# Layer 1 of a two-layer attention kernel: the last chunk's sums move to TensorE, the value biases move into the residual, and VectorE joins two groups of rows in eight products with addition

## The chip, the cores and the metric

The kernel runs on one core of a Trainium2 chip. A core has a matrix engine (TensorE, PE in the profile, with its weight loads as PEld), a vector engine (VectorE, DVE), a scalar engine (ScalarE, ACT), a general engine (GpSimd, POOL) and SyncE (SP), whose queue issues most transfers here. The metric is device time in microseconds for one execution; smaller is better.

## What is computed

The input x has 2 images of 256 channels on 64 x 64 = 4096 positions, in float32. Two attention layers follow each other.

```python
# layer 0, per image: 4 heads of 16
xn  = layernorm(x)                      # over the 256 channels
att = softmax(q k^T / 4) @ v            # 4096 x 4096 scores per head
att = att * dyn[position]               # a gate from two small products on x
x1  = sigmoid(0.5 * (out_w att) + x)

# layer 1, per image: 4 heads of 64
q, k, v = w_qkv x1 + b_qkv              # v carries a bias of its own
att = softmax(q k^T / 8) @ v            # 4096 x 4096 scores per head
att = att.reshape(256, 4096)            # [head, position, d] read as [channel, position]
out = w_out att + b_out + x1
```

The reshape in layer 1 matters for the change: `(b, heads, position, d)` is read as `(b, channel, position)`. A row of the new 256 x 4096 array holds 64 positions of one head, each with its 64 values, so along the free axis a row repeats the 64 values of d 64 times. The softmax weights of a row add up to 1, so the value bias of head h adds the same 64 numbers to every position of that head.

## The kernel before: how the work is tiled and ordered

Layer 0 is streamed in steps of 128 keys and is not touched beyond its last stage, `finish` (L558): tanh on ScalarE, a scaling on GpSimd (L564), and a store of the finished 128 x 2 x 512 tile of x1 (L565). `layer1_constants` (L178) loads the weights and biases of layer 1 while layer 0 starts.

Layer 1 works in **units** (L769): one image b, one pair of heads g, one block j of 512 query positions. There are 2 x 2 x 8 = 32 units, in one long pipeline. A unit has 32 **chunks** of 128 keys, in two groups of 16; a **step** of the main loop (L1219) takes two chunks, so a unit starts every 16 steps. I call the step inside a unit its phase, 0 to 15. For one chunk and both heads:

- `score` (L850): TensorE makes a 128 x 2 x 512 tile of scores in PSUM (L861). Two such tiles rotate (pool `psp`), so the scores of a chunk wait until the copy of the chunk two before has been made.
- `keep` (L867): VectorE takes the running maximum over chunks (L878), then ScalarE copies the scores into one of 24 buffers in SBUF, the ring (L879).
- Twenty chunks (ten steps) later, when the group's maximum is known, `shift` (L942) subtracts it on VectorE (L944), and `weigh` (L951) takes the exponential on ScalarE (L956). It also adds the tile to the group's accumulator on GpSimd (L966 for the first sum, L968 after it): 15 additions per group of 16 chunks.
- `gather` (L970): TensorE multiplies the tile with the values (L978), into one PSUM bank per group.

Inside a step the program order is written out by hand (L1219 to L1247), and every engine works through its own instructions in that order: both scores; what hangs at "start" and "early"; the first chunk's keep, shift and exponential; what hangs at "early end"; the second chunk's keep; the two gathers; what hangs at "late" and "late end"; the second shift. Other work is hung on phases (L1109 to L1156): transposes of the maxima (L886) at phases 8 and 0, with VectorE's reductions (L898) behind them, their split into parts on GpSimd (L909 to L916), the turn on TensorE (L925) and the spread (L939); queries of the next unit at phases 14 and 15 (L672); keys and values of the next pair of heads at phases 4 to 7, only in the first 24 units.

The end of a unit runs ten steps into the next one. The groups' two halves are joined there:

- `total` (L998), phase 12: four products with ones (L1008) add the accumulators over the partitions, into the one bank `misc` (pool `psm`, one buffer; everything small uses it: keys, values, queries, transposes, output products).
- `factors` (L1029), phase 13: the reciprocal of the sums on VectorE, and a factor for each group.
- `turn_sums` and `rows` (L1042, L1045): the gathered values are transposed (L1023) into `misc`, and VectorE multiplies each by its factor (L1049): group 1 at the end of phase 13, group 0 at "early end" of phase 14. For group 1, GpSimd adds the value bias (L1056). For group 0, GpSimd adds the two halves (L1060; VectorE in the last unit). The rows then go to DRAM (L1076).

In the units that follow the first image, 16 output products hang as well (`project_out` and `output`, L1081 and L1089): TensorE at phases 3, 7, 11 and 15, and VectorE adds the output bias and x1 (L1091) at the end of the same step. The second image's outputs come at the very end, in `project_half` (L1192). For the last 20 chunks of the last unit `on_tensor` (L948) sends most sums to TensorE (L988) in place of GpSimd.

Of the kernel before, what the change touches and what calls it, by code (L numbers as in the profile page):

```python
# [27 lines left out]
def conv_attention_kernel(  # L28
# [57 lines left out]
    )  # L86
    x1 = [
        [dram.tile([C, NB], F32, tag=f"x1_{b}_{j}", name=f"x1_{b}_{j}") for j in range(NJ)]
        for b in range(B)
    ]  # L90
    att = [dram.tile([C, N], F32, tag=f"att_{b}", name=f"att_{b}") for b in range(B)]
# [86 lines left out]
    def layer1_constants():  # L178

        w1 = const.tile([P, CC, 3, C], F32, tag="w1", name="w1")  # L180
        for c in range(CC):
            for k in range(3):
                later_load(
                    w1[:, c, k, :].rearrange("p (h d) -> p h d", d=D1),
                    w_qkvT[c * P : (c + 1) * P, :].rearrange(
                        "p (h t d) -> p t h d", t=3, d=D1
                    )[:, k],
                )
        wo1 = later_load(
            const.tile([P, CC, C], F32, tag="wo1", name="wo1"), w_outT.rearrange(by_chunk, p=P)  # L190
        )

        b1 = const.tile([P, PR, 3], F32, tag="b1", name="b1")
        for k in range(2):
            later_load(
                b1[k * D1 : (k + 1) * D1],
                b_qkv_col.rearrange("d (g k t) -> d g k t", k=2, t=3)[:, :, k, :],
            )
        b1v = later_load(
            const.tile([P, H, D1], F32, tag="b1v", name="b1v"),  # L200
            b_qkv_row.rearrange("(h t d) -> t h d", t=3, d=D1)[2].partition_broadcast(P),
        )
        bo1 = later_load(const.tile([P, CC], F32, tag="bo1", name="bo1"), b_out)
        ident16 = const.tile([P, P], BF16, tag="ident16", name="ident16")
        nc.gpsimd.tensor_copy(ident16, ident)
        ones16 = const.tile([P, P], BF16, tag="ones16", name="ones16")
        nc.gpsimd.memset(ones16, 1.0)
        ones = const.tile([P, D1], F32, tag="ones", name="ones")
        nc.gpsimd.memset(ones, 1.0)


        negmax1 = []
        for i in range(2):
            t = const.tile([P, PB, P], BF16, tag=f"negmax1_{i}", name=f"negmax1_{i}")
            nc.gpsimd.memset(t, 0.0)
            negmax1.append(t)
        return w1, wo1, b1, b1v, bo1, ident16, ones16, ones, negmax1
# [27 lines left out]
    with own0:  # L245
# [306 lines left out]
        def add_x(u, c):  # L552
# [2 lines left out]
                xt[:, c, :], work.pop(("o", c)), gam, xt[:, c, :], ALU.mult, ALU.add  # L555
            ))

        def finish(u):  # L558
            b, j = u
            avs.pop(u)  # L560
            xt = res.pop(u)

            seq(nc.scalar.activation(xt, xt, AF.Tanh, scale=0.5))  # L563
            seq(nc.gpsimd.tensor_scalar(xt, xt, 0.5, 0.5, ALU.mult, ALU.add))  # L564
            nc.sync.dma_start(out=x1[b][j].rearrange("(c p) n -> p c n", p=P), in_=xt)  # L565


        for n, u in enumerate(units0):
# [87 lines left out]


        w1, wo1, b1, b1v, bo1, ident16, ones16, ones, negmax1 = layer1_constants()
        l1o = own1.enter_context(tc.tile_pool(name="l1o", bufs=1, side="right"))
        l1x = own1.enter_context(tc.tile_pool(name="l1x", bufs=2, side="right"))  # L660
        small_bank = [bank]
# [110 lines left out]
    LAG = GS // 2 + 2  # L772
    US = NM // 2
    END = len(units) * US


    LATE = len(units) * NM - 2 * LAG
    with (
# [172 lines left out]
        def weigh(t):  # L951
            u = b, g, j = units[t // NM]
            m = t % NM
            n = m // GS
            p = raws[t]
            seq(nc.scalar.activation(p, p, AF.Exp, scale=D1**-0.5))  # L956

            if on_tensor(t):
                return
            if (u, n) not in first:  # L960
                first[u, n] = p
            elif (u, n) not in accs:
                accs[u, n] = l1.tile(
                    [P, 2, NB], F32, tag="acc", bufs=3, name=f"acc_{b}_{g}_{j}_{n}"
                )
                seq(nc.gpsimd.tensor_tensor(accs[u, n], first[u, n], p, ALU.add))  # L966
            else:
                seq(nc.gpsimd.tensor_tensor(accs[u, n], accs[u, n], p, ALU.add))  # L968

        def gather(t):  # L970
            u = b, g, j = units[t // NM]
            m = t % NM
            n = m // GS
            if m % GS == 0:
                avs1[u, n] = psv.tile([P, NB], F32, tag="av", name=f"av1_{b}_{g}_{j}_{n}")
            v = vs[b, g, m // PB]
            for k in range(2):
                seq(nc.tensor.matmul(  # L978
                    avs1[u, n][k * D1 : (k + 1) * D1, :], v[:, m % PB, k, :], raws[t][:, k, :],
                    start=(m % GS == 0), stop=(m % GS == GS - 1),  # L980
                ))
            raws.pop(t - 1, None)
            if on_tensor(t):
                if u not in srows:
                    srows[u] = psp.tile([P, 2, NB], F32, tag="pair", name="late_sums")[:, 0, :]
                for k in range(2):
                    r = D1 * n + 32 * k
                    seq(nc.tensor.matmul(  # L988
                        srows[u][r : r + 32, :], ones[:, :32], raws[t][:, k, :],
                        start=r not in begun, stop=False, skip_group_check=True,  # L990
                    ))
                    begun.add(r)
            if m % GS == GS - 1:
                a = l1.tile([P, NB], F32, tag="avs", name=f"avs1_{b}_{g}_{j}_{n}")
                seq(nc.scalar.copy(a, avs1.pop((u, n))))
                avs1[u, n] = a

        def total(u):  # L998


            b, g, j = u
            late = u in srows
            if not late:
                srows[u] = misc(f"sum1_{b}_{g}_{j}")
            for n in range(NG):
                for k in range(2):
                    r = D1 * n + 32 * k
                    seq(nc.tensor.matmul(  # L1008
                        srows[u][r : r + 32, :], ones[:, :32], accs[u, n][:, k, :],
                        start=not late, stop=True, skip_group_check=late,  # L1010
                    ))

        def keep_total(u):
# [31 lines left out]
        def rows(u, n):  # L1045
            b, g, j = u
            ps = avs1.pop((u, n))
            r = l1.tile([P, PB, 2, D1], F32, tag="rows", name=f"rows_{b}_{g}_{j}_{n}")
            seq(nc.vector.tensor_tensor(  # L1049
                r, ps, joined[u][:, n].unsqueeze(3).to_broadcast([P, PB, 2, D1]), ALU.mult  # L1050
            ))
            last = u == units[-1]
            if n == 1:
                halves[u] = r
                bias = b1v[:, 2 * g : 2 * g + 2, :].unsqueeze(1).to_broadcast([P, PB, 2, D1])
                seq(nc.gpsimd.tensor_tensor(r, r, bias, ALU.add))  # L1056
                return
            joined.pop(u)
            engine = nc.vector if last else nc.gpsimd
            seq(engine.tensor_tensor(r, r, halves.pop(u), ALU.add))  # L1060


            if last:
# [24 lines left out]

        def output(b, j, o):  # L1089
            xt = loaded["xo", b, j]  # L1090
            seq(nc.vector.scalar_tensor_tensor(  # L1091
                xt[:, o, :], outs.pop((b, j, o)), bo1[:, o : o + 1], xt[:, o, :], ALU.add, ALU.add
            ))
            if o == CC - 1:
                nc.sync.dma_start(
                    out=out[b, :, bass.ts(j, NB)].rearrange("(c p) n -> p c n", p=P), in_=xt
                )

        def fetch_output(b, j):
            fetch(("xo", b, j), x1[b][j], "xo", 2, l1)  # L1100
            fetch(("ao", b, j), att[b][:, bass.ts(j, NB)], "ao", 1, l1)


# [5 lines left out]
        for n, u in enumerate(units):  # L1109
# [37 lines left out]
            if b < B - 1 and (g, j) == (PR - 1, NJ - 1):  # L1147
                for i in range(NJ):
                    t1 = t0 + US + (i + 4) * GS // 2
                    at(t1, "start", lambda b=b, i=i: fetch_output(b, i))  # L1150
                    for o in range(CC):
                        at(
                            t1 + 3 + 4 * o, ("early", "late")[o],
                            lambda b=b, i=i, o=o: project_out(b, i, o, misc(f"o1_{b}_{i}_{o}")),
                        )
                        at(t1 + 3 + 4 * o, "late end", lambda b=b, i=i, o=o: output(b, i, o))  # L1156

# [2 lines left out]
        def fetch_last(i):  # L1162
# [1 line left out]
            b = B - 1  # L1164
            tag, bufs, pool = (("xb", 3, l1x), ("xo", 2, l1), ("ao", 1, l1))[(i >= 3) + (i >= 5)]
            t = pool.tile([P, CC, NB], F32, tag=tag, bufs=bufs, name=f"x_last_{i}")
            nc.sync.dma_start(out=t, in_=x1[b][i].rearrange("(c p) n -> p c n", p=P))
            last_x.append(t)

        def fetch_first_half():  # L1170
# [5 lines left out]
        def last_output():  # L1176
# [9 lines left out]
            last_att.append(a)  # L1186
            for i in range(NJ - 2, NJ):
                t = tail.tile([P, CC, NB], F32, tag=f"xo{i}", name=f"x_last_{i}")
                nc.sync.dma_start(out=t, in_=x1[b][i].rearrange("(c p) n -> p c n", p=P))
                last_x.append(t)  # L1190

        def project_half(j, c, a):  # L1192
            ps = psp.tile([P, 2, NB], F32, tag="pair", name=f"o1_{c}_{j}")
            for o in range(CC):
                seq(nc.tensor.matmul(
                    ps[:, o, :], wo1[:, c, bass.ts(o, P)], a, start=True, stop=True
                ))
            for o in range(CC):
                x = last_x[j][:, o, :]
                if c == 0:  # L1200
                    seq(nc.vector.scalar_tensor_tensor(
                        x, ps[:, o, :], bo1[:, o : o + 1], x, ALU.add, ALU.add
                    ))
                else:
                    seq(nc.vector.tensor_tensor(x, ps[:, o, :], x, ALU.add))

        own_tail = ExitStack()
        for i in range(NJ - 2):
# [96 lines left out]
```

## Time and profile before

| what | value |
|---|---|
| median of 3 runs (lowest to highest) | 4742.49 us (4742.18 to 4742.60) |
| profiled execution: its own time / span of its trace | 4741.58 us / 4739.8 us |
| layer 1's first scores | 2058.0 us from the span's start |
| granted TensorE clock, mean | 0.996 |
| PE busy, whole span | 4526.9 us (96%) |
| VectorE busy, whole span | 3917.0 us (83%) |
| ScalarE busy, whole span | 3394.1 us (72%) |
| GpSimd busy, whole span | 2540.6 us (54%), of which L968 2098.1 us |

Times are microseconds from the start of the span unless marked ns. A group of instructions is one source line on one engine, with its operation and tile sizes; "busy" is the union of its instructions' times and "mean" the time of one. Matmuls appear as two instructions each in float32 (x4 for two products). In a timeline, a row is one instruction or a run of like ones without a pause ("x8"), with the idle time before it and what ended it in brackets. In the chain of waits each row names the work on which the next row waited, and "issue" is time in which nothing that the profile shows was waited for. A releaser is inferred: where an instruction waits for several engines, the profile names the one whose signal came last before the start, whether or not that signal was needed.

### The profile page before, as it was taken

The numbers are of one execution on the slowest core, as the hardware profiler recorded it, in microseconds if no ns is written. First come the engines' busy times: TensorE is split into PE (matmuls) and PEld (weight loads), VectorE is DVE, ScalarE is ACT, GpSimd is POOL, SyncE is SP. The second block draws the span as 40 slices with busy tenths as digits, with TensorE's granted clock in tenths as the row PEclk, the third lists the DMA queues.
The fourth block names the chain that finished last, engine by engine and source line by source line (L and its number), as shares of the span: only waits on it lengthen the run. The fifth ranks groups of instructions, "written<-read, shape, count | busy, mean of one in ns | idle before, by whom it ended". The sixth has DMA issues, their size and how long they took to land.

```text
span 4739.8 us, 70643 instructions
## 1 busy us (share of the span) xinstructions
PE 4526.9 (96%) x27506; PEld 1496.2 (32%) x27506; DVE 3917.0 (83%) x4584; ACT 3394.1 (72%) x4508; POOL 2540.6 (54%) x1491
## 2 busy tenths in 40 slices
PE   8999999999999999989999999999999999999998
PEld 3433333333333333333232232323233332222222
DVE  6777777777777777359999999999999899999996
ACT  3366666666666666668888888888887778888884
POOL 6300000000000000039999999999998889999994
PEclk9999999999999999999999999999999999999999
DMA  3100000000000000110000100001111111000002
GB/s 103 34 4 19 19 21 15 15 15 15 15 15 15 15 13 13 57 63 25 23 25 17 54 30 23 25 23 36 52 36 45 63 52 47 18 14 7 14 16 74
DMA packets 113381, 140.10 MB, mean 30 GB/s; under 512 B 51864, under 2 KB 52696, under 8 KB 112932
## 3 DMA queue, kind: packets, MB, share of 16 engines
q1 hardware_dynamic: 111260, 135.11, 9.2%
q8 instruction: 216, 3.54, 0.3%
q14 instruction: 121, 0.99, 0.1%
q10 hardware_dynamic: 1784, 0.46, 0.0%
HBM read 93.58 MB, written 41.70 MB: 29 GB/s over the span
## 4 chain that ended last, share of the span: by engine, by line
PE 58%; DVE 15%; POOL 15%; issue 6%; ACT 5%; DMA 1%; SPq 0%; ACTq 0%; DVEq 0%; POOLq 0%
PE s L448 24%; POOL acc L968 13%; PE av L463 12%; DVE rmax L878 10%; PE s L861 6%; PE av L978 5%; DVE raw L944 4%; ACT raw L879 4%; PE a L410 2%; PE p L270 1%; PE k1p L672 1%; POOL acc L966 1%; PE rt L886 1%; PE q1p L672 1%; PE o L549 1%
## 5 line engine op out<-in xcount | busy, mean ns | idle before, releaser
L968 POOL TENSOR_TENSOR acc<-acc,raw 128x1024 f32<-128x1024 f32 x884 | 2098.1, 2373 | 89.4 <-ACT raw L956 30.2
L414 DVE TENSOR_REDUCE mx<-a 128x1 f32<-128x512 f32 x2048 | 1315.3, 686 | 450.5 <-PE a L410 449.4
L451 ACT ACTIVATE p<-s 128x512 f32<-128x512 f32 x2048 | 1109.8, 597 | 701.3 <-PE a L410 367.3
L944 DVE TENSOR_TENSOR raw<-raw,shift 128x1024 f32<-128x1024 f32 x1024 | 1238.0, 1213 | 19.2 <-PE shift L939 12.7
L861 PE MATMUL s<-q,k 64*128 64x512 f32 x4096 | 1117.2, 636 | 142.9 <-ACT raw L879 134.6
L878 DVE TENSOR_TENSOR rmax<-s,rmax 128x1024 f32<-128x1024 f32 x960 | 1170.1, 1219 | 72.7 <-PE s L861 70.8
L879 ACT COPY raw<-s 128x1024 f32<-128x1024 f32 x1024 | 1037.7, 1013 | 259.4 <-DVE rmax L878 173.5
L448 PE MATMUL s<-q,kT 32*128 32x512 f32 x4096 | 1219.1, 640 | 0.0
L956 ACT ACTIVATE raw<-raw 128x1024 f32<-128x1024 f32 x1024 | 1086.9, 1062 | 178.4 <-DVE raw L944 147.3
L410 PE MATMUL a<-kT,q 32*128 32x512 f32 x4096 | 1129.7, 643 | 1.2 <-DVE mx L414 1.0
L978 PE MATMUL av<-raw,v 128*64 128x512 f32 x4096 | 999.3, 606 | 2.0
L463 PE MATMUL av<-p,v 128*32 128x256 f32 (+1 forms) x7904 | 650.2, 399 | 0.6 <-ACT avs L477 0.6
L861 PEld LDWEIGHTS s<-q,k 64*128 64x128 f32 x4096 | 317.1, 185 | 827.9 <-ACT raw L879 628.0
L513 POOL TENSOR_TENSOR f<-f,dyn 128x16 f32<-128x16 f32 x15 | 3.3, 223 | 1028.2 <-DVE f L512 1028.2
L448 PEld LDWEIGHTS s<-q,kT 32*128 32x128 f32 x4096 | 397.9, 183 | 426.3 <-issue 392.1
L978 PEld LDWEIGHTS av<-raw,v 128*64 128x64 f32 x4096 | 243.3, 136 | 587.6 <-issue 428.8
L463 PEld LDWEIGHTS av<-p,v 128*32 128x32 f32 x7904 | 157.6, 108 | 751.5 <-issue 737.3
L564 POOL TENSOR_SCALAR res<-res 128x1024 f32<-128x1024 f32 x16 | 16.8, 1049 | 660.5 <-ACT res L563 660.5
L410 PEld LDWEIGHTS a<-kT,q 32*128 32x128 f32 x4096 | 305.0, 184 | 31.4 <-DVE mx L414 18.2
L966 POOL TENSOR_TENSOR acc<-raw,raw 128x1024 f32<-128x1024 f32 x64 | 152.4, 2381 | 112.7 <-ACT raw L956 103.8
L898 DVE TENSOR_REDUCE negs<-rt 128x4 f32<-128x512 f32 x128 | 88.3, 690 | 50.1 <-PE rt L886 47.6
L318 DVE RECIPROCAL std<-std 128x128 f32<-128x128 f32 x64 | 56.1, 920 | 37.7 <-ACT std L313 37.7
(332 smaller groups left out, 1840.4 us busy)
## 6 DMA issues: line engine op xcount, KB each, us to landing
x<-in_x_dram SPq DMA_DIRECT2D x16, 512.0 KB
res<-in_x_dram SPq DMA_DIRECT2D x16, 512.0 KB
x<-res SPq DMA_DIRECT2D x16, 512.0 KB
att<-rows SPq DMA_DIRECT2D x62, 128.0 KB
kd<-k1s SPq DMA_DIRECT2D x24, 256.0 KB
vd<-v1s SPq DMA_DIRECT2D x24, 256.0 KB
k<-kd SPq DMA_DIRECT2D x24, 256.0 KB
v<-vd SPq DMA_DIRECT2D x24, 256.0 KB
```

The source lines that it names most:

```text
L410: seq(nc.tensor.matmul(ps, qs0[u][r, bass.ts(i, P)], kTs[b][r, bass.ts(m, NB)], start=True, stop=True,))
L414: seq(nc.vector.tensor_reduce(mxs[u][:, i * H + h, m : m + 1], ps, AX.X, ALU.max))
L448: seq(nc.tensor.matmul(ps, kTs[b][r, bass.ts(m, P)], qs0[u][r, :], start=True, stop=True))
L451: seq(nc.scalar.activation(pt[:, k, :], ps, AF.Exp, scale=D0**-0.5))
L463: seq(nc.tensor.matmul(avs[u][32 * h : 32 * h + 32, cols], vs0[b][:, m, 32 * h : 32 * h + 32], pts[t, h // 2][:, h % 2, cols], start=(m == ...
L861: seq(nc.tensor.matmul(ps[:, k, :], ks[b, g, m // PB][r, bass.ts(m % PB, P)], qs1[u][r, :], start=True, stop=True,))
L878: seq(nc.vector.tensor_tensor(rmax[u, n], ps, before, ALU.max))
L879: seq(nc.scalar.copy(raw, ps))
L944: seq(nc.vector.tensor_tensor(raws[t], raws[t], shifts[u, t % NM // GS], ALU.add))
L956: seq(nc.scalar.activation(p, p, AF.Exp, scale=D1**-0.5))
L968: seq(nc.gpsimd.tensor_tensor(accs[u, n], accs[u, n], p, ALU.add))
L978: seq(nc.tensor.matmul(avs1[u, n][k * D1 : (k + 1) * D1, :], v[:, m % PB, k, :], raws[t][:, k, :], start=(m % GS == 0), stop=(m % GS == GS ...
```

## The change

Four things change together.

1. The sums of each unit's last chunk (m = 31) leave GpSimd. Two products with ones on TensorE, behind that chunk's gather in phase 10, add it into `misc` directly. The bank is therefore taken at phase 10 and not at phase 12, and `total` adds the accumulators to it.
2. The value bias leaves `rows`. It is multiplied with w_out once, in layer 0 (`make_bias` on TensorE, `keep_bias` on ScalarE, which adds the output bias too), and `finish` stores a second copy of x1 with that bias added (`xb1`; one GpSimd addition of 128 x 1024 and one store of 512 KB per block). The outputs read `xb1`, so that they need only an addition.
3. In `rows`, the two halves are no longer added by GpSimd. Group 0 no longer gets a product and an addition; VectorE makes eight scalar_tensor_tensor instructions of 128 x 64 instead, each a product with a per-partition factor and an addition to group 1's row.
4. The output products of odd blocks move from phases 11 and 15 to 10 and 15, and the first of each two is added at "early end", so that `misc` is free again when the sums take it. In `project_half` two VectorE instructions of 512 become one of 1024.

```diff
+        def make_bias():
+            ps = bank("bias")
+            for o in range(CC):
+                for c in range(CC):
+                    seq(nc.tensor.matmul(
+                        ps[:, bass.ts(o, D1)], wo1[:, c, bass.ts(o, P)], b1v[:, c, :],
+                        start=(c == 0), stop=(c == CC - 1),
+                    ))
...
         def finish(u):
             nc.sync.dma_start(out=x1[b][j].rearrange("(c p) n -> p c n", p=P), in_=xt)
+            xb = l0w.tile([P, CC, NB], F32, tag="xb", bufs=1, name=f"xb1_{b}_{j}")
+            seq(nc.gpsimd.tensor_tensor(
+                xb.rearrange("p c (s d) -> p c s d", d=D1),
+                xt.rearrange("p c (s d) -> p c s d", d=D1),
+                bias.unsqueeze(2).to_broadcast([P, CC, NB // D1, D1]),
+                ALU.add,
+            ))
+            nc.sync.dma_start(out=xb1[b][j].rearrange("(c p) n -> p c n", p=P), in_=xb)
...
         def weigh(t):
-            if on_tensor(t):
+            if on_tensor(t) or m == NM - 1:
                 return
...
         def gather(t):
-            if on_tensor(t):
+            if on_tensor(t) or m == NM - 1:
                 if u not in srows:
-                    srows[u] = psp.tile([P, 2, NB], F32, tag="pair", name="late_sums")[:, 0, :]
+                    if t >= LATE:
+                        srows[u] = psp.tile([P, 2, NB], F32, tag="pair", name="late_sums")[:, 0, :]
+                    else:
+                        srows[u] = misc(f"sum1_{b}_{g}_{j}")
                 for k in range(2):
                     r = D1 * n + 32 * k
                     seq(nc.tensor.matmul(
                         srows[u][r : r + 32, :], ones[:, :32], raws[t][:, k, :],
-                        start=r not in begun, stop=False, skip_group_check=True,
+                        start=(u, r) not in begun, stop=False, skip_group_check=True,
                     ))
...
         def rows(u, n):
-            r = l1.tile([P, PB, 2, D1], F32, tag="rows", name=f"rows_{b}_{g}_{j}_{n}")
-            seq(nc.vector.tensor_tensor(
-                r, ps, joined[u][:, n].unsqueeze(3).to_broadcast([P, PB, 2, D1]), ALU.mult
-            ))
             if n == 1:
+                r = l1.tile([P, PB, 2, D1], F32, tag="rows", name=f"rows_{b}_{g}_{j}")
+                seq(nc.vector.tensor_tensor(
+                    r, ps, joined[u][:, n].unsqueeze(3).to_broadcast([P, PB, 2, D1]), ALU.mult
+                ))
                 halves[u] = r
-                bias = b1v[:, 2 * g : 2 * g + 2, :].unsqueeze(1).to_broadcast([P, PB, 2, D1])
-                seq(nc.gpsimd.tensor_tensor(r, r, bias, ALU.add))
                 return
-            joined.pop(u)
-            engine = nc.vector if last else nc.gpsimd
-            seq(engine.tensor_tensor(r, r, halves.pop(u), ALU.add))
+            f, r = joined.pop(u), halves.pop(u)
+            for i in range(PB):
+                for k in range(2):
+                    seq(nc.vector.scalar_tensor_tensor(
+                        r[:, i, k, :], ps[:, i, k, :], f[:, n, i, k : k + 1], r[:, i, k, :],
+                        ALU.mult, ALU.add,
+                    ))
...
         def output(b, j, o):
-            seq(nc.vector.scalar_tensor_tensor(
-                xt[:, o, :], outs.pop((b, j, o)), bo1[:, o : o + 1], xt[:, o, :], ALU.add, ALU.add
-            ))
+            seq(nc.vector.tensor_tensor(xt[:, o, :], outs.pop((b, j, o)), xt[:, o, :], ALU.add))
...
+                        step = t1 + (3 - i % 2, 7)[o]
                         at(
-                            t1 + 3 + 4 * o, ("early", "late")[o],
+                            step, ("early", "late")[o],
...
         def project_half(j, c, a):
+            seq(nc.vector.tensor_tensor(last_x[j], ps, last_x[j], ALU.add))
```

The value biases are also loaded differently (four small loads in place of one), and `total` starts a group of sums only where the last chunk has not begun it.

## Prediction

> **What bounds the kernel now.** I read the page first. Its busy shares do not settle anything: in layer 1 PE, VectorE and GpSimd all stand at 9 tenths. Its chain of waits puts 13% of the span on GpSimd's additions (L968), which would make this change a good one. So I asked for busy time over three single units, cut from one step of a unit to the same step of the next (columns: window, its length, then busy time and instruction count of PE, PEld, VectorE, ScalarE, GpSimd):
>
> ```profile
> 2825.00:2906.30 81.30, 76.70 (x330) 24.34 (x332) 76.35 (x72) 68.50 (x75) 75.54 (x43) 1.00 0.07 23
> 3649.50:3738.30 88.80, 83.69 (x346) 27.45 (x346) 79.08 (x77) 68.74 (x74) 75.45 (x43) 1.00 0.18 57
> 4151.70:4230.90 79.20, 72.83 (x310) 21.64 (x310) 76.05 (x73) 67.97 (x71) 75.44 (x43) 1.00 0.04 11
> ```
>
> The first is a common unit, the second also makes output products, the third makes no keys and values. GpSimd does the same 75.5 us in all three, while the period moves from 79.2 to 88.8 with PE's work. GpSimd cannot set a period that varies like that. Next I asked what GpSimd waits for (2400 to 3400 us, 12.3 units; total us, times, longest):
>
> ```profile
> POOL acc L966 <- ACT raw L956: 43.2, 25, 2.5
> ```
>
> It idles 43.2/12.3 = 3.5 us a unit, always for the first exponentials of a group: it catches up twice a unit. The lines of the turn on TensorE (L925) name who waits for GpSimd's split:
>
> ```profile
>   POOL negmax L912: 23.4, 24
> ```
>
> That counts weight loads and products both; PE itself idles 0.53 a unit there, and I come back to it. ScalarE's copy (L879) and VectorE's shift (L944) are also put down to L968, but I checked the need: the copy of chunk t may overwrite the ring's buffer once the addition of chunk t-24 has ended. Pairing both lines' rows in order, that margin is never under 2.5 us in the whole layer, and GpSimd is at most 2.6 us behind the exponentials. GpSimd blocks nobody there.
>
> What is left is a loop of VectorE, ScalarE and PE. The chain of waits through the end of a unit (start, length, what):
>
> ```profile
> 2846.27 0.60 DVE rows L1049
> 2846.87 1.14 DVE rmax L878
> 2848.11 1.02 ACT raw L879
> ...
> 2849.18 1.13 PE s L861 x4
> 2850.31 1.06 PE q1p L672 x2
> 2851.37 1.87 PE av L978 x8
> 2853.23 2.03 PE s L861 x8
> 2855.26 0.59 PE rt L886 x4
> ```
>
> The group-0 row product (L1049) stands on the chain itself: behind it come the maximum, the copy that frees the score buffer, the next scores, and then PE without a pause until VectorE waits for the transposes. A microsecond more at L1049 is a microsecond more per unit. TensorE's q1p waits there too: it takes the bank `misc` that the row product reads (its weight load waits for L1049 10.7 us over 12 units).
>
> **The change, part by part.**
>
> *Eight products (31 units, phase 14, on the path).* No row shows a vector instruction of 64 elements with a per-partition factor. The nearest are the same operation on 512 elements and the plain one:
>
> ```profile
> 4661.17 1.40 DVE L1201 SCALAR_TENSOR_TENSOR x_last<-o,bo,x_last 128x512 f32<-128x512 f32 x2
> 4724.11 1.29 DVE L1205 TENSOR_TENSOR x_last<-o,x_last 128x512 f32<-128x512 f32 x2 [0.43 <-PE o L1195]
> ```
>
> One of L1201 lasts 0.745, two last 1.40 to 1.41: an independent successor starts 0.665 after the first (L1205: 1.29 less 0.69 is 0.60). L944 of 1024 elements advances 1.133, so 512 elements cost 1.133 - 0.60 = 0.533, or 1.04 ns each. For 64: 0.665 - 448 x 1.04 ns = 0.199. Eight: 1.59. L1049's product of 0.60 goes. **Net +0.99 us a unit.** Bounds: without the factor's extra 0.065, 8 x 0.134 = 1.07, net +0.47. If each waited for the one before, as L1035 to L1038 do (start to start 0.19 to 0.20 at a duration of 0.16, so 0.035 behind the end), 8 x (0.278 + 0.035) = 2.5, net +1.9. I take 0.99: the two L1201 write slices of one tile, as the eight do, and overlap. Queued behind them on VectorE are the maximum, shift and the next step; PE's scores wait for those, as the chain shows.
>
> [...]
>
> *Sums of the last chunk on PE (31 units, phase 10).* The row of the same two products:
>
> ```profile
> 4663.78 1.05 PE L988 MATMUL late_sums<-raw,ones 128*32 128x512 f32 x4
> ...
> 2826.77 1.13 PE L861 MATMUL s<-q,k 64*128 64x512 f32 x4
> 2828.61 1.13 PE L861 MATMUL s<-q,k 64*128 64x512 f32 x4 [0.72 <-ACT raw L879]
> ```
>
> In a run the four instructions advance PE by 0.98. They come between the gather and the scores at 2826.77. Those scores would then start at 2827.75, and VectorE's maximum, which starts 1.18 after its scores' start where PE is late (as at 2838.22, idle 0.60), at 2828.93; before, it ran at 2828.48. So 0.53 of 0.98 is hidden by VectorE's backlog. **Net +0.45 a unit**; below, 0 if the backlog is larger; above, 0.98. `total` keeps its four products. The bank `misc` is free in time: ScalarE's copy of the turn (L930) ends in phase 10 some 2.7 us before the sums.
>
> *What leaves GpSimd.* One addition (2.37) and two row additions (1.29, 1.28): 4.9 us a unit. By the margins above nobody waits for them, except the split. The turn's wait, 0.53 in phase 1, goes, since GpSimd lags less there; but behind it PE waits 0.34 for the copy before its second scores, and VectorE is not idle then, so I cost the gain at 0, at most 0.5 a unit. VectorE's L944 advances 1.13 whether GpSimd runs (2842) or rests (4668), so nothing gets faster by GpSimd's rest.
>
> *Outputs.* 16 additions lose the factor: 16 x 0.065 = -1.0. Four odd blocks move from phase 11 to 10, where the spread (L939) and VectorE's shift then stand behind 1.9 us of output products, and the sums behind VectorE's addition. Working those two steps through by their rows, PE's next-but-one scores come about 0.75 later than the sums alone explain: +3 (estimate, 0 to 8).
>
> *Layer 0.* PE hardly rests there; four small products, at L1023's 0.15 an instruction x 8, at most 1.2: I take +0.7. `finish`'s addition (2.37, as L968) lies on an idle GpSimd. The second store waits for it on SP's queue; the loads behind it (queries, residuals, sums) are asked for steps ahead. At the start of layer 1 a buffer that the last `xb` holds until about 2065.5 could delay a ring copy: 0, at most 3.
>
> *The end.* `project_half` saves 0.1 to 0.2 in two or three places on VectorE's way to the last rows. The last unit's eight products (1.6) replace two instructions (0.60 + 0.69), and the first row's store can go when its slice is done, about 1 us earlier. -1.5 (0 to -2.5).
>
> *Sum against the profiled execution's 4741.6:* 31 x (0.99 + 0.45) = 44.6; + 3 + 0.7 - 1.0 - 1.5 = **45.8**; 4741.6 + 45.8 = **4787**. The median of the runs is 0.9 higher than that execution, which is nothing beside the range. About 0.2%, or 9.5 us, is what a measurement of this kernel can tell from no change.
>
> **The rivals.**
>
> *GpSimd is the bound after all (faster).* For it: the chain gives POOL's additions 43% of the window from 2800 to 2990. If that is real, the 4.9 us taken off count for 43%, -2.1 a unit, and the added 1.44 for the other 57%, +0.8: -1.3 x 31 = -40, so 4702. It decides from the point where the ring margin reaches zero; the trace shows 2.5 us at least, and one GpSimd load at three periods. Chance 0.09.
>
> *Cover (no change).* VectorE idles 4.7 us a unit, 0.98 of it shortly after the products, and PE idles 0.94 and 0.72 around phase 10. If these took both additions whole, 4742. Against it: those idle times are where VectorE waits for PE, and PE was late through this very chain. Chance 0.05.
>
> *Dear products (slower still).* The eight serialise: 4741.6 + 31 x (1.9 + 0.45) + 1.2 = 4816. Against it: the overlapping pairs. Chance 0.12.
>
> *Cheap or half hidden.* Products at 0.134, or the sums wholly behind the backlog: 31 x 0.47 + 1.2 = 16 at the lowest (4757), 31 x (0.47 + 0.45) + 1.2 = 30 (4771). Chance 0.10.
>
> **How the numbers follow.** Forecast 4787, with 4772 to 4802 of its own: 0.64. The range takes in the half hidden and dear cases from 4760 to 4816 and leaves out the two other rivals and the tails: about 0.8. Faster 0.09, same 0.05, slower 0.86.
>
> **What would show it.** Common units should last 82.7, those without keys and values 80.6. The products: eight instructions of 0.28, 0.2 apart, with VectorE's maximum right behind and q1p about 1 us later. Phase 11: VectorE's first maximum waits for scores about 0.45. GpSimd: 70.6 us busy a unit and more idle, with nobody faster. I am wrong if a common unit stays at or under 81.3, or if VectorE's idle time shrinks by as much as its work grows.

## The result, and the profile after

The changed kernel takes **4795.87 us** (median of 4 runs, 4794.74 to 4796.41) against 4742.34 (4741.69 to 4742.60) for the kernel before, run beside it: a ratio of 1.0113 [1.0101, 1.0125]. It is slower, by 53.5 us; 45.8 more than the profiled execution had been forecast. The profiled execution of the changed kernel took 4794.74 us with a span of 4792.9; the two spans differ by 53.1.

The lines of the two kernels differ, so here are the names that matter: scores L902 (before L861), maximum L919 (L878), copy L920 (L879), shift L985 (L944), gather L1019 (L978), GpSimd's first sum L1007 and its additions L1009 (L966, L968), queries L712 (L672). New are the last chunk's sums L1032 and the eight products L1099. I write `e1` to `e11` for the experiments' kernels.

Busy time of the changed kernel in three single units, cut as before from a unit's first shift to the next unit's (window, its length, then PE, PEld, VectorE, ScalarE, GpSimd):

```profile
2841.38:2924.08 82.70, 77.31 (x334) 24.47 (x334) 77.38 (x79) 68.59 (x74) 70.69 (x39) 1.00 0.07 23
3683.20:3774.25 91.05, 85.29 (x350) 27.44 (x350) 79.79 (x83) 68.70 (x73) 70.52 (x39) 1.00 0.17 55
4194.35:4275.00 80.65, 73.51 (x314) 21.79 (x314) 77.12 (x80) 68.06 (x71) 70.69 (x40) 1.00 0.04 11
```

GpSimd has lost 4.9 us a unit, and all three kinds of unit have become longer: a common one 82.70 (before 81.30), one with output products 91.05 (88.75 in steady state), one without keys and values mostly 80.59 (79.19). PE and VectorE have gained busy time, 0.6 and 1.0 in the common unit.

What GpSimd waits for from 2400 to 3400 us (total, times, longest):

```profile
POOL acc L1007 <- ACT raw L997: 89.9, 24, 5.0
POOL acc L1009 <- ACT raw L997: 24.8, 24, 1.4
```

Before, it idled 43.2 us in this stretch; now it idles 114.7. The relief became idle time.

The chain of waits through the join of two groups (start, length, what):

```profile
2943.93 0.60 PE turned L1063 x4
...
2945.72 1.54 DVE rows L1099 x8
2947.26 1.14 DVE rmax L919
...
2948.50 1.02 ACT raw L920
...
2949.57 1.13 PE s L902 x4
2950.70 1.05 PE q1p L712 x2
2951.75 1.87 PE av L1019 x8
```

This is the chain that the prediction showed, with 1.54 us of products where one product of 0.60 stood. The maximum, the copy and the scores follow one another as before, later by the difference. On PE's own timeline (start, duration) the query product followed the gather without a pause before:

```profile
2844.99 1.94 PE L978 MATMUL av<-raw,v 128*64 128x512 f32 x8
2846.93 1.12 PE L672 MATMUL q1p<-b_('q', (0, 1, 2))_23813,w 128*128 128x512 f32 x2
```

Now it pauses. The profile names no releaser; the products, which read the bank that it takes, end at 2947.26, 0.1 before it starts:

```profile
2944.45 1.94 PE L1019 MATMUL av<-raw,v 128*64 128x512 f32 x8
2947.36 1.10 PE L712 MATMUL q1p<-b_('q', (0, 1, 3))_24416,w 128*128 128x512 f32 x2 [0.98 <-issue]
```

The sums of the last chunk, some 20 us before that join, first on PE and then what VectorE sees of them:

```profile
2925.77 1.05 PE L1032 MATMUL sum<-raw,ones 128*32 128x512 f32 x4
2926.75 2.00 PE L902 MATMUL s<-q,k 64*128 64x512 f32 x8
```

```profile
2927.93 1.23 DVE L919 TENSOR_TENSOR rmax<-s,rmax 128x1024 f32<-128x1024 f32 x1 [0.36 <-PE s L902]
```

The sums advance PE by 0.98. VectorE waits 0.36 for the scores behind them; before, it had no pause at this place:

```profile
2828.48 1.22 DVE L878 TENSOR_TENSOR rmax<-s,rmax 128x1024 f32<-128x1024 f32 x1
```

### The profile page after: what moved, and what is told of

Same layout as the page of the kernel before. It is cut to its first block, busy times and chain, and to the rows that moved or that the text cites. A ratio compares the mean times of both kernels' runs of the same rounds, so it can differ in the third digit from the quotient of the medians.

```text
span 4792.9 us, 71068 instructions
## 1 busy us (share of the span) xinstructions
PE 4553.3 (95%) x27638; PEld 1501.5 (31%) x27638; DVE 3946.4 (82%) x4791; ACT 3395.5 (71%) x4510; POOL 2427.8 (51%) x1413
## 4 chain that ended last, share of the span: by engine, by line
PE 65%; DVE 19%; issue 8%; ACT 6%; POOL 2%; DMA 1%; ACTq 0%; DVEq 0%; SPq 0%; POOLq 0%
PE s L458 24%; PE av L473 12%; DVE rmax L919 12%; PE s L902 9%; PE av L1019 7%; DVE raw L985 5%; ACT raw L920 5%; PE a L420 2%; POOL acc L1009 1%; PE rt L927 1%; PE p L280 1%; DVE rows L1099 1%; PE k1p L712 1%; PE q1p L712 1%; PE v1p L745 1%
## 5 line engine op out<-in xcount | busy, mean ns | idle before, releaser
L1009 POOL TENSOR_TENSOR acc<-acc,raw 128x1024 f32<-128x1024 f32 x853 | 2022.9, 2372 | 155.3 <-ACT raw L997 95.1
L902 PE MATMUL s<-q,k 64*128 64x512 f32 x4096 | 1113.1, 635 | 155.1 <-ACT raw L920 145.4
L985 DVE TENSOR_TENSOR raw<-raw,shift 128x1024 f32<-128x1024 f32 x1024 | 1237.0, 1212 | 28.0 <-PE shift L980 21.7
L920 ACT COPY raw<-s 128x1024 f32<-128x1024 f32 x1024 | 1036.8, 1012 | 306.4 <-DVE rmax L919 226.6
L919 DVE TENSOR_TENSOR rmax<-s,rmax 128x1024 f32<-128x1024 f32 x960 | 1169.5, 1218 | 80.6 <-PE s L902 77.9
L1019 PE MATMUL av<-raw,v 128*64 128x512 f32 x4096 | 1002.4, 607 | 2.0
L902 PEld LDWEIGHTS s<-q,k 64*128 64x128 f32 x4096 | 317.0, 185 | 837.4 <-ACT raw L920 610.9
L1019 PEld LDWEIGHTS av<-raw,v 128*64 128x64 f32 x4096 | 243.8, 136 | 587.3 <-issue 433.2
L1007 POOL TENSOR_TENSOR acc<-raw,raw 128x1024 f32<-128x1024 f32 x64 | 152.1, 2377 | 243.5 <-ACT raw L997 243.5
```

Source lines behind the costliest of these rows:

```text
L902: seq(nc.tensor.matmul(ps[:, k, :], ks[b, g, m // PB][r, bass.ts(m % PB, P)], qs1[u][r, :], start=True, stop=True,))
L919: seq(nc.vector.tensor_tensor(rmax[u, n], ps, before, ALU.max))
L920: seq(nc.scalar.copy(raw, ps))
L985: seq(nc.vector.tensor_tensor(raws[t], raws[t], shifts[u, t % NM // GS], ALU.add))
L1019: seq(nc.tensor.matmul(avs1[u, n][k * D1 : (k + 1) * D1, :], v[:, m % PB, k, :], raws[t][:, k, :], start=(m % GS == 0), stop=(m % GS == GS ...
```

## Experiments

My theory: the period is a loop of PE, VectorE and ScalarE; the eight products and the sums each lengthen it, and GpSimd's relief is worth nothing. The rival: GpSimd sets part of the period, so that its relief pays back some of a larger cost. Each kernel was timed beside the kernel before; "ratio" is to it. Three kernels (e4, e8, e9) start from the kernel before, the others from the changed one.

**e1_products_back: the rows joined as before.** The eight products go; VectorE's product and GpSimd's addition return (VectorE's in the last unit).

```diff
-            for i in range(PB):
-                for k in range(2):
-                    seq(nc.vector.scalar_tensor_tensor(
-                        r[:, i, k, :], ps[:, i, k, :], f[:, n, i, k : k + 1], r[:, i, k, :],
-                        ALU.mult, ALU.add,
-                    ))
+            r = l1.tile([P, PB, 2, D1], F32, tag="rows", name=f"rows_{b}_{g}_{j}_{n}")
+            seq(nc.vector.tensor_tensor(
+                r, ps, f[:, n].unsqueeze(3).to_broadcast([P, PB, 2, D1]), ALU.mult
+            ))
+            engine = nc.vector if last else nc.gpsimd
+            seq(engine.tensor_tensor(r, r, other, ALU.add))
```

> The changed kernel, but the two groups' rows are joined as before: one product of 128 x 512 on VectorE and one addition of 128 x 512 on GpSimd; the rest of the change stays. If the price of the change is VectorE's loop, the eight products' 1.53 us a unit become 0.60 again and 30 joins each give back 0.93: 4796 - 28 = 4768, and a common unit lasts 81.8. About 2 us more go at the end of the run, where the eight products let TensorE wait for 2.1 us and its granted clock was 0.5 for 3.4 us: 4766. If GpSimd were the bound, its 1.29 us more a unit would make this slower than 4796. If the sums on TensorE were the main price, this would stay within 10 us of 4796.

Measured: 4764.58 us, ratio 1.0048 [1.0033, 1.0063]; a common unit 81.73. The products cost 82.70 - 81.73 = 0.97 a unit. A common unit of this run (columns as above):

```profile
2178.51:2260.24 81.73, 77.32 (x334) 24.48 (x334) 76.43 (x73) 68.56 (x74) 71.89 (x40) 1.00 0.08 23
```

**e2_sums_back: the last chunk's sums back on GpSimd.**

```diff
-            if on_tensor(t) or m == NM - 1:
+            if on_tensor(t):
```

This goes for both places, the exponential's and the gather's, and `total` takes the bank again.

> The changed kernel, but the last chunk's sums are GpSimd's again; products, biases and output phases stay as changed. VectorE's loop: 0.98 us less on TensorE in phase 10, of which 0.45 was not hidden, so 31 x 0.45 = 14 us less, and some 2 to 3 us less in the four units with output products in phase 10: 4780. A common unit lasts 82.25. GpSimd as the bound: 2.37 us more a unit, slower than 4796 by up to 70. TensorE's whole 0.98 on the path: 4796 - 30 = 4766.

Measured: 4781.40, ratio 1.0085 [1.0069, 1.0100]; a common unit 82.23. The sums cost 82.70 - 82.23 = 0.47.

```profile
2838.02:2920.25 82.23, 76.59 (x330) 24.33 (x330) 77.28 (x80) 68.40 (x74) 73.08 (x40) 1.00 0.08 23
```

**e3_both_back: both edits.** What stays is the value bias in the residual, the new output phases and the shorter end.

> The changed kernel with both undone: what stays is the bias by way of the residual, the second store of x1, and the output products' new phases. If the two prices add, 4796 - 28 - 2 - 14 - 3 = 4749, with common units at 81.3 as before; what is left over 4742 is the start of layer 1 (first ring copy 6.3 us later, first shift 3.8 us later than before). If they overlap, more than 4755. GpSimd as the bound: slower than the changed kernel.

Measured: 4751.95, ratio 1.0022 [1.0013, 1.0032]; a common unit 81.28, as before the change. The two costs add up: 0.97 + 0.47 = 1.44 against 82.70 - 81.28 = 1.42. What is left lies in the output units and at the start.

```profile
2831.72:2913.00 81.28, 76.64 (x330) 24.35 (x330) 76.32 (x73) 68.41 (x74) 74.18 (x41) 1.00 0.08 23
```

**e4_relief_only: the kernel before, with GpSimd relieved and nothing added.**

```diff
-            if on_tensor(t):
+            if on_tensor(t) or m == NM - 1:
                 return
...
-                bias = b1v[:, 2 * g : 2 * g + 2, :].unsqueeze(1).to_broadcast([P, PB, 2, D1])
-                seq(nc.gpsimd.tensor_tensor(r, r, bias, ALU.add))
...
-            seq(engine.tensor_tensor(r, r, halves.pop(u), ALU.add))
+            halves.pop(u)
```

> The kernel before, with GpSimd relieved and nothing put in place: the last chunk's additions, the value biases and the join of the two groups are left out (so the output lacks them). GpSimd does 4.9 us less a unit, VectorE and TensorE do what they did. VectorE's loop: 4742, within 4; common units stay at 81.3. GpSimd as the bound, even in part: by its share of the chain (43%), 2.1 us a unit less, 4677; wholly, 4620.

Measured: 4741.15, ratio 1.0000 [0.9990, 1.0010]. Its common unit:

```profile
2825.30:2906.58 81.28, 76.64 (x332) 24.34 (x330) 76.32 (x73) 68.41 (x74) 70.69 (x39) 1.00 0.08 23
```

GpSimd is at 70.69 where the kernel before had 75.54, and the period is 0.02 shorter. The units without keys and values are the stronger case: there GpSimd is busy 75.44 of 79.19 us, more than PE (72.82), and they too stay, at 79.17. This rules out the rival: GpSimd's relief by these additions is worth nothing.

**e5_xb_in_res: the new tile in other memory.** The changed kernel's first copy into the ring waits for the store of the last `xb` tile (ScalarE's timeline):

```profile
2057.64 1.06 ACT L592 ACTIVATE res<-res 128x1024 f32<-128x1024 f32 x1 [1.06 <-DVE res L564]
2065.52 1.01 ACT L920 COPY raw<-s 128x1024 f32<-128x1024 f32 x1 [6.82 <-DMA xb<-xb]
```

Before, that copy waited for its scores alone:

```profile
2059.24 1.01 ACT L879 COPY raw<-s 128x1024 f32<-128x1024 f32 x1 [0.30 <-PE s L861]
```

The edit puts the tile into another pool:

```diff
-            xb = l0w.tile([P, CC, NB], F32, tag="xb", bufs=1, name=f"xb1_{b}_{j}")
+            xb = res_pool.tile([P, CC, NB], F32, tag="xb", bufs=1, name=f"xb1_{b}_{j}")
```

> The changed kernel, but the tile from which the second copy of x1 is stored lies in the pool of the residuals and not behind the working tiles of layer 0, so that the ring of layer 1 does not take its place. If the late start is that one buffer, the first ring copy starts at about 2059 and not 2065.5, the first shift is back at 2095, and the run loses 4 to 5 us: 4791. If the store's traffic or the queue is what delays layer 1, nothing moves: 4796. Common units stay at 82.7.

Measured: 4792.32, ratio 1.0108 [1.0091, 1.0125]. The time came out near the expected one, but not by the expected way: the first shift is at 2098.08, not 2095. The copy came 2.7 earlier and now waits for GpSimd's addition; then VectorE waits for the same store:

```profile
2065.67 1.22 DVE L919 TENSOR_TENSOR rmax<-s,raw 128x1024 f32<-128x1024 f32 x1 [7.54 <-DMA xb<-xb]
```

So in both places the layer-1 tile that takes the memory of the last `xb` waits for its store. The intervals of the two ratios overlap, so that the gain of 3.5 us is at the edge of what the times can tell; in the profiles only 0.9 of it comes from the start; most of the rest is the end (113.00 from the last unit's first shift, against 114.94), where a gather that takes 1.94 in this execution took 3.54 in the changed kernel's, at a granted clock of 0.50.

**e6_bias_only: e3 with the outputs at their old phases.**

```diff
-                        step = t1 + (3 - i % 2, 7)[o]
...
-                            step, ("early", "late")[o],
+                            t1 + 3 + 4 * o, ("early", "late")[o],
...
-                            step, ("early end", "late end")[o],
-                            lambda b=b, i=i, o=o: output(b, i, o),
+                        at(t1 + 3 + 4 * o, "late end", lambda b=b, i=i, o=o: output(b, i, o))
```

> The kernel before with the bias by way of the residual alone: joins, sums and output phases are those of before. Against the run with both parts undone (4752, whose units with output products last 90.0) this has the old output phases back: if these are what made those units longer than 88.75, four units give back 1.2 to 2.8 each, and this is 4745 to 4747, of which 4 to 6 over before are the late start. If the bias by way of the residual costs something in the output units itself, they stay at 90.0 and this is 4752.

Measured: 4747.01, ratio 1.0012 [1.0003, 1.0022]; a unit with outputs takes 88.60, in e3 89.97. The new phases cost 1.37 in such a unit and, by the two medians, 4.9 us in all. The bias by way of the residual saves 0.15 there (88.75 before) and costs the late start: first shift at 2099.49, against 2095.20. Of the kernels tried that leave nothing of the work out, this one is the nearest to the kernel before, and still slower.

**e7_sixteen: sixteen products of 32 elements in place of eight of 64.**

```diff
-                    seq(nc.vector.scalar_tensor_tensor(
-                        r[:, i, k, :], ps[:, i, k, :], f[:, n, i, k : k + 1], r[:, i, k, :],
...
+                    for d in (slice(0, D1 // 2), slice(D1 // 2, D1)):
+                        seq(nc.vector.scalar_tensor_tensor(
+                            r[:, i, k, d], ps[:, i, k, d], f[:, n, i, k : k + 1], r[:, i, k, d],
...
```

> The changed kernel with sixteen products of 128 x 32 in place of eight of 128 x 64: the same elements, twice the instructions. If an instruction advances VectorE by 0.13 fixed and 1.04 ns an element, sixteen take 16 x 0.164 = 2.6 us in place of 1.53, and a common unit lasts 82.7 + 1.1 = 83.8: 4796 + 31 x 1.1 = 4830. If the price is in the elements, or in PSUM reads, nothing moves: 4796. If each instruction waited for the one before, the eight would already show it, and sixteen would take 16 x 0.28 = 4.5: 4888.

Measured: 4852.70, ratio 1.0235 [1.0220, 1.0251]: 23 more than expected. The products take 2.53 (1.54), and a unit without disturbance 83.68, which is 0.98 more and near the expected 1.1. But from the ninth to the seventeenth every unit takes 85.33 or 85.45, and some others 1.2 to 1.7 more than undisturbed. PE's pause at the query product has grown to 1.98 us, and the granted clock (third last column, after PEld, VectorE, ScalarE and GpSimd) drops behind it:

```profile
2959.90:2963.32 3.42, 1.44 (x7) 0.41 (x4) 3.42 (x18) 1.58 (x2) 3.34 (x2) 1.00 0.01 2
2963.32:2966.73 3.41, 3.41 (x8) 0.90 (x9) 1.92 (x2) 2.07 (x2) 1.15 (x2) 0.50 0.38 77
```

PE was busy 1.44 of 3.42 us, and the next 3.41 ran at half clock (0.50). That costs 85.33 - 83.68 = 1.65 in such a unit. Over all disturbed units of the profiled execution (4848.67) it comes to some 23; with 31 x 0.98 for the products these are the 54 that it takes longer than the changed kernel's.

**e8_more_gpsimd: the kernel before, with GpSimd burdened.** Two more passes over the rows behind the value bias, one adding the bias, one taking it off.

```diff
+                for op in (ALU.add, ALU.subtract):
+                    seq(nc.gpsimd.tensor_tensor(r, r, bias, op))
```

> The kernel before with more work for GpSimd: it adds the value bias once more and subtracts it again, two passes of 128 x 512 at 1.28 us in each unit, behind the first. GpSimd idles 3.5 us a unit, so VectorE's loop gives 4742 as long as the turn's wait for the split stays behind TensorE's other waits: up to 0.5 us a unit more, 4742 to 4757. GpSimd as the bound: 2.57 us more a unit, 4742 + 31 x 2.57 = 4822.

Measured: 4834.79, ratio 1.0197 [1.0182, 1.0213]: a clear miss. 2.6 us more on GpSimd cost 2.1 to 4.3 us in a common unit and 3.3 to 4.6 in one without keys and values, but nothing in a steady unit with output products (88.72). GpSimd's timeline (start, duration) and PE's show where:

```profile
2789.63 2.63 POOL L1058 TENSOR_TENSOR rows<-rows,b1v 128x512 f32<-128x512 f32 x2
...
2798.23 9.70 POOL L968 TENSOR_TENSOR acc<-acc,raw 128x1024 f32<-128x1024 f32 x4
2807.87 0.21 POOL L909 CAST negmax<-negs 128x8 bf16<-128x8 f32 x1
```

```profile
2809.02 0.61 PE L925 MATMUL nm1p<-ident,negmax 128*128 128x128 bf16 x4 [3.21 <-POOL negmax L912]
2809.56 3.79 PE L861 MATMUL s<-q,k 64*128 64x512 f32 x8
```

GpSimd does not pause between the join and the split (L909 to L912) that PE's turn needs. So the 2.6 us arrive whole at PE, which waited 0.53 there and now waits 3.21; and the eight matmuls behind it take 3.79 at half clock (granted 0.50 from 2807.57 to 2814.40) in place of some 2.0.

**e9_more_in_pause: as much work, put into GpSimd's pause before a new group.** Two passes over the gathered values of group 0, each a product with ones, at phase 10.

```diff
+            if u != units[-1]:
+                at(t1 + 2, "late end", lambda u=u: more(u))
```

> The kernel before with the same extra work for GpSimd as in the last run (two passes of 128 x 512 a unit, here a product with ones that changes nothing), but hung on phase 10, behind the unit's last addition, where GpSimd waits 2.54 us for the next group's first exponential. If what cost 93 us there was only the split, queued behind the passes at phase 14 and 15 while TensorE waited 3.2 us for it, this stays near the kernel before: 4742 to 4750, common units 81.3 to 81.5. If GpSimd's work as such is on the path, wherever it is put, this is as slow as there: 4820 to 4835.

Measured: 4760.33, ratio 1.0039 [1.0025, 1.0054]. This is over the expected 4742 to 4750, but far under 4820. The common units are at 81.28: there the work is free. Nearly all of the 19 us come from the last units, without keys and values, which rise from 79.2 to 80.6 to 82.3. In the kernel before, GpSimd's pause is 0.5 us there (2.5 in a common unit); now the split is late again (L909 at 4193.07), PE waits 1.78 for it, and the clock falls:

```profile
4191.61:4195.02 3.41, 1.63 (x10) 0.53 (x8) 3.14 (x3) 3.22 (x4) 3.19 (x7) 1.00 0.00 0
4195.02:4198.43 3.41, 3.41 (x12) 1.01 (x10) 1.27 (x2) 2.04 (x3) 3.33 (x2) 0.50 0.00 0
```

**e10_two_ops: VectorE joins with two long instructions, a product and an addition.** As e1, but the addition stays on VectorE in every unit.

> The changed kernel with the join made by VectorE in two instructions of 128 x 512 (product, then addition) in place of eight of 128 x 64. Two advance VectorE by 2 x 0.60 = 1.20, eight by 1.53: a common unit lasts 82.7 - 0.33 = 82.4 and the run 4796 - 31 x 0.33 = 4786. If the fixed part of an instruction is not what the eight cost, this is as slow as they are or slower: two passes over 512 elements in place of one.

Measured: 4802.24, ratio 1.0129 [1.0113, 1.0144]; a common unit 82.91: slower than with eight products, where 82.4 had been expected. VectorE's timeline (start, duration):

```profile
2947.59 0.68 DVE L1098 TENSOR_TENSOR rows<-turned,f 128x512 f32<-128x512 f32 x1
2948.30 1.26 DVE L1101 TENSOR_TENSOR rows<-rows,rows 128x512 f32<-128x512 f32 x1
2949.49 1.21 DVE L919 TENSOR_TENSOR rmax<-s,rmax 128x1024 f32<-128x1024 f32 x1
```

The addition takes 1.26 where the same one in the last unit, with GpSimd idle, takes 0.69. Its neighbour on GpSimd:

```profile
2946.64 5.14 POOL L1009 TENSOR_TENSOR acc<-acc,raw 128x1024 f32<-128x1024 f32 x2 [0.84 <-ACT raw L997]
```

In all 31 units in which GpSimd works, the addition ends 0.545 to 0.554 us after the GpSimd addition that ran when it began, which still had 0.70 to 0.72 to go. GpSimd's next addition takes 2.68 to 2.70, not 2.37. So each took longer beside the other. By what, the runs do not show: GpSimd always had about the same time to go. The wait between product and addition is small beside it: 0.71 from start to start, where independent ones have 0.60 to 0.67. In all VectorE needs 1.90 (2947.59 to 2949.49) where the eight products need 1.54; of these 0.36 the period gets 0.21, probably because the query product on PE, which waits for the product only, has no pause any more; no run tests that.

**e11_sums_between: the sums between the two scores of phase 11,** where PE waits 0.7 for a copy, and not ahead of both.

```diff
+                if t >= LATE:
+                    add_sums()
+                else:
+                    at((t + 2 * LAG + 1) // 2 + 1, "between", add_sums)
...
-            scores = [score(c) for c in pair] if inside else []
+            scores = [score(pair[0])] if inside else []
+            hung(t, "between")
+            if inside:
+                scores.append(score(pair[1]))
```

> The changed kernel with the last chunk's sums moved on TensorE by one place: from behind the gather of phase 10 to between the two scores of phase 11, where TensorE waits 0.72 us for ScalarE's copy. The same 0.98 us then ends 0.25 later than the copy, and VectorE's maximum for those scores has that much backlog: nothing of it is left on the path, a common unit lasts 82.7 - 0.47 = 82.2 as without the sums, and the run 4796 - 14 = 4782. If the sums cost by TensorE's total and not by where they stand, 4796 again.

Measured: 4781.76, ratio 1.0086 [1.0069, 1.0103]; a common unit 82.23, exactly e2's. On PE the sums now fill the wait between the two scores:

```profile
2921.22 1.13 PE L902 MATMUL s<-q,k 64*128 64x512 f32 x4
2922.28 1.05 PE L1035 MATMUL sum<-raw,ones 128*32 128x512 f32 x4
2923.26 1.13 PE L902 MATMUL s<-q,k 64*128 64x512 f32 x4
```

The sums themselves cost nothing; their place costs 0.47.

## Why the prediction was right, and which terms were off

*What bounds it.* Right. e4 takes GpSimd from 75.5 to 70.7 us a unit and the period stays, even in the units where GpSimd is busy 95% of it; the additions that the chain gave to GpSimd (15% of the span before, 2% after) were never to be had. The prediction's reading by three single units, the busy time of a true bound has to move with the period, holds.

*Eight products.* Predicted 8 x 0.199 = 1.59, net 0.99; measured 1.54 and, by e1, 0.97. The eight overlap, as the prediction took from the pairs of L1201: they start 0.19 apart at a duration of about 0.28, so that none waits for the end of the one before, which had been put at net 1.9.

*Sums.* Predicted 0.45; measured 0.47 by e2, with VectorE's pause of 0.36 as the new wait. The half that VectorE's backlog was to hide is hidden.

*What leaves GpSimd.* Predicted 0, at most 0.5 from the split; measured 0.00. The turn's wait of 0.53 does go, and PE waits 0.94 for the copy behind it (0.33 before), as the prediction put it. Before and after:

```profile
2862.92 0.40 PE L925 MATMUL nm1p<-ident,negmax 128*128 128x128 bf16 x4 [0.54 <-POOL negmax L912]
2863.25 1.13 PE L861 MATMUL s<-q,k 64*128 64x512 f32 x4
2864.71 1.13 PE L861 MATMUL s<-q,k 64*128 64x512 f32 x4 [0.33 <-ACT raw L879]
```

```profile
2880.03 0.40 PE L966 MATMUL nm1p<-ident,negmax 128*128 128x128 bf16 x4
2880.35 1.13 PE L902 MATMUL s<-q,k 64*128 64x512 f32 x4
2882.42 1.13 PE L902 MATMUL s<-q,k 64*128 64x512 f32 x4 [0.94 <-ACT raw L920]
```

What the prediction did not see is the other side: e8 shows that the same place has no cover against more GpSimd work.

*Outputs.* Predicted +3 and -1.0. Measured: the output units lose 3.6 beyond the common 1.4 each, so +2 net had been forecast and 3.6 came. e6 parts it: about 4.9 for the new phases in e3, 0.15 a unit saved by the shorter addition. Why the phases cost less beside the joins and sums of the changed kernel, no run shows.

*Start of layer 1.* This is the term that was mis-sized most: predicted "0, at most 3", measured 5.1. The place was named, and the store did land at 2065.5; the first copy started 6.3 later than before, of which 3.8 are left at the first shift. In e4, e8 and e9, which have no `xb`, the first shift is at 2093.9 to 2094.8 (2095.2 before). The other 1.3 is the first window (80.80, before 79.47) and need not come from the change: e4, which has no `xb`, shows 80.79 too, with a stretch at half clock at the same place (in the changed kernel 2103.46 to 2106.87, granted 0.50).

*The end.* Predicted -1.5; measured +0.85 beyond the last join's 1.40. The products make PE wait 2.13 us for a copy in the last unit (1.19 before), and the gather behind it runs at half clock (granted 0.50 from 4704.41 to 4707.82):

```profile
4703.46 1.18 PE L902 MATMUL s<-q,k 64*128 64x512 f32 x4 [2.13 <-ACT raw L920]
4704.56 3.54 PE L1019 MATMUL av<-raw,v 128*64 128x512 f32 x8
```

That is 3.54 for eight where 1.94 is usual. In e5 the wait is the same and the gather takes its usual time:

```profile
4701.99 1.13 PE L902 MATMUL s<-q,k 64*128 64x512 f32 x4 [2.13 <-ACT raw L920]
4703.05 1.94 PE L1019 MATMUL av<-raw,v 128*64 128x512 f32 x8
```

There the end is 1.1 better than the join alone explains (113.00 - 112.69 - 1.40), near the -1.5. That the shorter code gave this is not shown: e5's stretch at half clock ahead of the last output products is also 3.41 shorter (10.24 us, 13.65 in the other two), and e3 and e6, which have the shorter `project_half` and the old joins, end at 112.81 and 113.49, no earlier than the kernel before.

*Layer 0.* Predicted +0.7; layer 1's first scores start 0.25 earlier than before, which the start's 5.1 already contains.

The sum: 30 x 1.405 + 1.40 for the joins = 43.55; + 3.6 + 5.1 + 0.85 = 53.1, as between the spans. The 7 us between forecast and result are the start and the end (5.1 + 2.35). The other differences cancel by luck: joins -1.05 (44.6 forecast), outputs +1.6, layer 0 -0.7. How the late start could be avoided is open: the one other place that was tried for the tile only moved the wait.

## What to carry to other kernels

Before taking work off an engine that looks 93% busy, compare units of different length: if its busy time stays while the period moves, it probably does not set the period, and e4 is the cheap test (leave the work out and add nothing). For work that goes from such an engine to one in the loop, the place can count more than the length: the sums cost 0.47 ahead of both scores and nothing between them. And an engine with idle time is not free everywhere: ask, for every place, who waits for what comes behind it in its queue.

## What the runs showed of the hardware

**In these runs the clock of PE halved behind short pauses.** The granted clock is 1.0 or 0.5 in the records, and in the kernel before and the changed one all its changes lie whole multiples of 3.413 us apart; stretches at half clock that end inside the record last 3.41, 6.83, 13.65 or 17.07. In the steady part, half clock came behind stretches of this grid in which PE was busy 1.51 of 3.42 us (changed kernel, 2100.04 to 2103.46, a pause of 1.91), 1.28 of 3.41 (the same, 4701.00 to 4704.41, a pause of 2.13), 1.44 (e7, a pause of 1.98), 1.58 (e8, 2804.16 to 2807.57, a pause of 3.21 that ran on into the next) and 1.63 (e9, a pause of 1.78). The least that the kernel before had there was 2.31 (4462.65 to 4466.06, and 1.00 granted behind it), and it has no half clock from 2069.90 to 4708.40. Where a pause fell made a difference: in e5 the wait of 2.13 is divided between two stretches, with 2.98 and 1.72 busy, and no half clock follows. Nor is it a sharp limit: five stretches of 1.43 to 1.62 in e7 and e9 were not followed by half clock, and one of 1.51 at the start of the changed kernel's layer 1 (2059.09 to 2062.50) was not either. That the clock goes by PE's share of such a stretch is the author's estimate from these cases.

**In e7 the clock and the loop kept step.** Nine units in a row last 85.33 us (one 85.45), which is 25 x 3.413, and not the 83.68 of the undisturbed ones: the stretches at half clock come 85.33 apart, so that the pause meets the same place of the grid again in every unit.

**In e10 VectorE and GpSimd each took longer beside the other.** VectorE's addition of two tiles in SBUF took 1.26 beside a busy GpSimd and 0.69 with GpSimd idle, GpSimd's next addition 2.68 to 2.70 and not 2.37. The eight products of the changed kernel read one of their two tiles from PSUM and show none of it: 0.19 apart beside a busy GpSimd (1.62 for all eight), and 0.19 apart at the very end, where GpSimd rests (1.61, at 4756.72). Whether the memory makes the difference, no run shows.
